# A factorization kernel on one core: bias loaded last, two load queues, P2 in its own bank, 12-bit parts by adding DMAs, unscaled banks

## The chip, the cores and the metric

The kernel runs on one core of a Trainium2 chip. The metric is the device time of one execution in microseconds (us). The core's engines are TensorE (PE, matmuls; PEld is its weight load), VectorE (DVE), ScalarE (ACT), GpSimd (POOL) and SyncE (SP, which here only issues transfers). Matmul results land in PSUM banks, everything else lies in SBUF or in device memory.

## The reference

```python
out_lin = x @ lin_w.T + lin_b                       # x 1024x512, lin_w 512x512
xv = jnp.einsum('bf,efm->bem', x, weight)           # weight 64x512x512
zp = jnp.einsum('bf,efm->bem', jnp.square(x), jnp.square(weight))
interaction = 0.5 * jnp.sum(jnp.square(xv) - zp, axis=1)
return out_lin + interaction
```

All is fp32. Nearly all of the work is xv, 64 products of 1024x512 by 512x512, squared and summed over the 64. zp needs only the sum of the squared weights over e, so it is one product at the end.

## The kernel before, in words

**Seven products in place of eight.** Every large product is done as a 2x2 block product in the Strassen-Winograd form: seven block products P1 to P7 of sums of the blocks. The left operands are quarters of x (A11, A12, A22, also X1, X2, X4) and four sums of them (R5, R6, R3, R7, also X5, X6, X3, X7). The right operands are the weight quarters w11, w21, w22, a running sum T (which takes quarter after quarter and serves P5, P6 and P4), and w12 after w22 was added to it (P7).

**Stages.** First the linear part x @ lin_w.T (`one_level` in lines 485 to 513: matmuls L494 where it goes by k, L507 elsewhere), which runs in plain fp32 and leaves its four quarters in device memory (`lin_copy`, `lin_add`, `lin_store`). Then 32 half groups (16 groups of columns times two halves of NCB), each with the seven products in the order P1, P6, P2, P3, P7, next half group's P5, P4 (`ORDER`); their matmuls are L678. Last the tail, which multiplies the squares of x by the sums of the squared weights (`one_level` again, L507), adds the accumulated interaction and the linear part to it (`into`), and stores.

**A product of a half group** (`product`, line 670). Fp32 operands are split into 12-bit parts so that PE can take them in its faster fp32r type: H (leading), L (rest) and K (a combination of both that makes up for the cross terms). A product is a front, H·H and L·L, and a back, K·K, which comes `LAG` = 4 slots later; between them the bank is scaled by 1 + 2^-12 and takes its addend (`stt`, L349; `dve`, L355; L712). In half group 0 the products P1, P2, P4 (`PLAIN`) are done in plain fp32. The 12-bit parts of x (`x_pieces`, line 471) are made once; those of the weights (`split`, line 612) for every product: pH and pL by ACT (L343), then pL by a POOL subtraction (L361) or by a DMA that adds (L380), and pK by POOL.

**Banks.** Four double banks go round in a ring. Each product has two halves (of 256 rows of x each), each half with a double bank. So P4's second half takes the double bank that P7's second half had.

**What reads a bank.** After the back, `finish` (line 663) has ACT square the bank (sq<-bank) and DVE reduce it into acc. P7's bank has a second reader: DVE's w<-bank−p5 (lines 727 and following), the addend of P4. Two instructions of different engines that read the same bank run one after the other, in the order in which they are emitted.

**Order of the work.** Nothing is emitted directly. Every operation is put on a `Plan` with its cost on its engine and what it reads and writes. `deadlines` gives each its latest start, counted back from the chain of matmuls, whose order is fixed by their keys. `forward` then simulates the engines: each takes, of what is ready, the operation with the earliest latest start. Loads on SP are not issued more than `AHEAD` = 50 us before that. `order` repeats this 60 times with shifted due times (`urge`) and keeps the one that ends first; instructions are emitted in that order. `both` marks DVE instructions that share a port with POOL. `landing` tells the plan when a load at the start is taken to arrive.

Of the kernel before, what the change touches and what calls it, by code (L numbers as in the profile page):

```python
# [19 lines left out]
U = 2.0 ** -12  # L20
S = 2.0 ** 12
TRIM = 1.0 - 2.0 ** -13

PLAIN = (1, 2, 4)
LAG = 4
ORDER = (1, 6, 2, 3, 7, 5, 4)
SPLIT = {**dict.fromkeys(range(1, 8), "POOL"), 5: "DMA", 3: "DMA"}
SCALE = {1: "DVE", 5: "ACT"}
# [5 lines left out]
PE, DVE, ACT, POOL, SP = "PE", "DVE", "ACT", "POOL", "SP"  # L34
NONE = ""


class Plan:
    HOP = 0.3
    OWN = 0.05  # L40
    AHEAD = 50.0
    ROUNDS = 60
    SEED = 0
    DEPTH = 8
    YIELD = 0.0

    def __init__(self):
        self.ops = []
# [91 lines left out]
    def forward(self, chain):  # L140
# [3 lines left out]
        free = dict.fromkeys(pending, 0.0)  # L144
        running = dict.fromkeys(pending)
        times = [self.HOP]
        done, late, nxt, wire, held = [], 0.0, 0, [9.0], None

        def release(o):
            for e in o.costs:  # L150
# [24 lines left out]
        def pick(e, now):  # L175
            if e == PE:
                if nxt < len(chain):
                    o = chain[nxt]
                    if not left[o.n] and ready(o, PE) <= now + 1e-6:
                        return o  # L180
                return None
            at = {n: ready(ops[n], e) for n in pending[e]}
            for n in sorted((n for n in at if at[n] <= now + 1e-6),
                            key=lambda n: (ops[n].latest, n)):
                o = ops[n]
                if e == SP and o.latest - self.AHEAD > now + 1e-6:
                    heapq.heappush(times, o.latest - self.AHEAD)
                    return None
                until = now + o.costs[e]
                if not any(  # L190
                    now + 1e-6 < at[u] < until - 0.2
                    and ops[u].latest < o.latest
                    and ops[u].latest + late < until + 0.1
                    for u in at
                ):
                    return o
            return None
# [43 lines left out]
def kernel(  # L241
# [5 lines left out]
    lin_b: bass.AP,  # L247
    out: bass.AP,
):

# [87 lines left out]
    def f32(n):  # L338
        return buf[n].bitcast(F32)
# [60 lines left out]
    def landing(name, at):  # L400
        plan.add({SP: 0.0}, None, (), (name,), land=at - 2 * plan.HOP)
# [16 lines left out]
        for z in ks:  # L418
            landing((n, z % KH, c), at)

    load_x("A11", 0, 0, 1, 3.5)
    load_lw(nc.scalar, [0], 0, 3.5)
    load_x("A11", 0, 1, 2, 3.9)
    load_lw(nc.scalar, [1], 0, 5.2)
    load_x("A11", 1, 0, 2, 5.0)
    load_lw(nc.scalar, [2, 3], 0, 7.2)
    load_x("A12", 0, 0, 2, 6.4)
    load_x("A12", 1, 0, 2, 7.4)
    load_lw(nc.sync, [0, 1], 1, 8.4)
    load_lw(nc.sync, [2, 3], 1, 9.2)  # L430
    for at, (n, k) in enumerate((("A22", 0), ("A22", 1), ("A21", 0), ("A21", 1))):
        load_x(n, k, 0, 2, 10.0 + 0.8 * at)
    nc.scalar.dma_start(bias[:], lin_b)
    landing("bias", 9.5)
    nc.scalar.preload_act_table(AF.Square)

    def a_parts(*names):
# [31 lines left out]
    x_sum("R7", "A11", "A21", "a - b", ("R7",))  # L469
    x_sum("R3", "R6", "A12", "-a - b", ("R3",))  # L470
    def x_pieces(i):
        n, (h, l, k) = OPERAND[i], (f"X{i}{z}" for z in "HLK")
        act(buf[h], buf[n], AF.Copy, a_parts(n), (h,), scale=S * TRIM)
        stt(buf[l], buf[n], S, f32(h), ALU.subtract, a_parts(n) + (h,), (l,), 1024, True)
        stt(buf[k], f32(h), -U, f32(l), ALU.add, (h, l), (k,), 1024, True)

    for i in (5, 6, 3, 7, 1, 2, 4):
        x_pieces(i)
# [3 lines left out]
    def four():  # L482
        return [both_of(banks()) for _ in range(4)]
# [33 lines left out]
        r.update({p: (t[k], t_names[k]) for p, k in ((5, 1), (6, 2), (7, 3), (4, 4))})  # L517
        return r

    f1, f4, f3, f2 = four()  # L520
    zero = nc.const_aps.tensor(0.0, [P, N])
    for u in range(2):
        nc.tensor.matmul(
# [16 lines left out]
        dma(lin_dram[:, ts(c, 2), ts(h, H)], buf[n], ((n, 0), (n, 1)), (("lind", h, c),))  # L540

    one_level(1, lin_rhs, lhs, f1, True, -1000, True)
    for u in range(2):
        act(buf[f2[u]], buf[f1[u]], AF.Copy, (f1[u],), (f2[u],), 512)
    one_level(2, lin_rhs, lhs, f1, False, -990, True)
    lin_copy("L11", f1, 0, 1.0)
    lin_store("L11", 0, 0)
    one_level(4, lin_rhs, lhs, f4, True, -980)
    one_level(5, lin_rhs, lhs, f3, True, -970)
    buf["L22"] = buf["A21"]  # L550
    used(("L22", 0), ("L22", 1), *a_parts("A21"))
    lin_copy("L22", f3, 1, -1.0)
    one_level(6, lin_rhs, lhs, f2, False, -960)
# [5 lines left out]
    lin_copy("L12", f2, 1, -1.0)  # L559
    one_level(3, lin_rhs, lhs, f3, False, -950)  # L560
    lin_add("L12", f3, True)
    lin_store("L12", 0, 1)
    one_level(7, lin_rhs, lhs, f2, False, -940)
    lin_add("L22", f2, True)
    lin_store("L22", 1, 1)
    lin_add("L21", f2, False)
    lin_store("L21", 1, 0)


# [26 lines left out]
    def load_more(h, n, q):  # L596

        o = now[h, n]
        if h:
            dma_add(buf[o], src(h, q), (), (o,))  # L600
        else:
            i = now[h, QUAD[q]]
            pool(buf[o], buf[o], buf[i], False, (o, i), (o,))
# [24 lines left out]
    def prepare(h, p):  # L628
        if p == 5:
            load(h, "T", 0)  # L630
            if h:
                load_more(h, "T", 1)
                load(h, "w11", 0)
            load(h, "w12", 1)
            if not h:
                load_more(h, "T", 1)
                load(h, "w11", 0)
                load(h, "w22", 3)
                load(h, "w21", 2)
# [17 lines left out]
        return n if not h and p in PLAIN else split(n, SPLIT[p] if h else POOL)  # L657

    acc_name = {}
    value = {}  # L660
# [191 lines left out]
    one_level(6, right, left, f2, False, key + 8)  # L852
    for u in range(2):
        into(z, f2, True, u)
        n = o_name[0, 1]
        dve(buf[n, u], buf[n, u], buf[z, u], True, ((n, u), (z, u)), ((n, u),), 512, True)
    one_level(7, right, left, f2, False, key + 11)
    for u in range(2):
        into(y, f2, True, u)
# [3 lines left out]
        into(o_name[1, 0], f2, True, u)  # L863
    one_level(3, right, left, f4, True, key + 14)
    for u in range(2):
        into(o_name[0, 1], f4, True, u)
# [52 lines left out]
```

## Time and profile before

| | us |
|---|---|
| median of 3 runs | 1298.06 |
| lowest and highest of them | 1298.05, 1299.3 |
| profiled execution, its own time | 1299.58 |
| profiled execution, its span | 1297.6 |

The mean granted TensorE clock of the profiled execution is 0.999. In the rows that follow, a line such as "L343 ACT ACTIVATE sq<-bank" is a group of instructions by source line, engine, operation and tiles (output on the left). In a timeline row the first number is the start in us from the start of the span, the second the time it took, and the bracket at the end says how long the engine had been idle and what released it. In a table of waits stand the total in us, the number of waits and the longest. In the table by stretches each engine has its busy time and number of instructions, and the granted clock, the share of the DMA engines and GB/s follow. In the chain of waits, each row is a start, a duration and what the end of the program went through. Line 343 is every ACT instruction, 349 every `stt`, 355 every `dve`, 361 every `pool`, 368 every `reduce`, 375 every `dma`, 380 every `dma_add`, so tiles tell them apart. Several tiles have two names there: w, p, sq and T are also the homes of x's quarters and of the lin weights at the start.

### The profile page before, as it was taken

How to read it: one execution, taken by the hardware profiler on the slowest of the kernel's cores; microseconds unless marked ns; L12 is line 12 of the kernel's file. 1: busy time of each engine (PE TensorE's matmuls, PEld its weight loads, DVE VectorE, ACT ScalarE, POOL GpSimd, SP SyncE). 2: the span in 40 equal slices, each digit the busy share in tenths (PEclk: the TensorE clock that was granted, in tenths of full speed). 3: DMA queues.
4: the chain of work that ended last, by engine and by line, in shares of the span. 5: the costliest groups of instructions: out<-in, count | busy, mean ns of one | idle time of the engine just before them, and what ended most of it. 6: DMA issues, size and time to landing. Idle time of an engine off the chain costs nothing.

```text
span 1297.6 us, 15705 instructions
## 1 busy us (share of the span) xinstructions
PE 1280.1 (99%) x5484; PEld 1026.0 (79%) x5484; DVE 1086.7 (84%) x954; ACT 1011.9 (78%) x1071; POOL 1095.3 (84%) x590
## 2 busy tenths in 40 slices
PE   8999999999999999999999999999999999999997
PEld 4668888888888888888888888888888888888873
DVE  4699888888888888888888888888888889888884
ACT  5568788788777888877888887788888788888872
POOL 3659898898888899889889888888988888998891
PEclk9999999999999999999999999999999999999999
DMA  6366676757667666677766666767667676766866
GB/s 226 97 164 160 155 170 150 158 129 154 163 155 167 142 152 145 149 163 164 162 147 143 153 151 161 167 145 161 133 148 168 147 162 152 169 131 144 184 130 150
DMA packets 75998, 200.25 MB, mean 154 GB/s; under 512 B 23824, under 2 KB 25104, under 8 KB 75920
## 3 DMA queue, kind: packets, MB, share of 16 engines
q0 software_dynamic: 28512, 101.72, 44.0%
q1 hardware_dynamic: 45552, 94.91, 22.6%
q10 hardware_dynamic: 1856, 2.62, 0.6%
q8 instruction: 43, 0.70, 0.2%
q14 instruction: 35, 0.29, 0.1%
HBM read 158.34 MB, written 6.29 MB: 127 GB/s over the span
## 4 chain that ended last, share of the span: by engine, by line
PE 92%; DMA 3%; DVE 2%; ACT 1%; issue 1%; POOL 1%; SPq 0%; DVEq 0%; ACTq 0%; POOLq 0%
PE bank L678 89%; PE bank L507 3%; DMA T<-weight 1%; DMA w<-weight 1%; DMA w<-xT 0%; PE bank L494 0%; DVE w L355 0%; POOL pL L361 0%; ACT sq L343 0%; ACT wsq L343 0%; POOL pK L361 0%; ACT pL L343 0%; DVE bank L355 0%; ACT bank L343 0%; DVE bank L349 0%
## 5 line engine op out<-in xcount | busy, mean ns | idle before, releaser
L361 POOL TENSOR_TENSOR pK<-pH,pL 128x1024 fp32r<-128x1024 f32 x221 | 560.1, 2554 | 19.8 <-PE bank L678 10.8
L343 ACT ACTIVATE sq<-bank 128x1024 f32<-128x1024 f32 x256 | 261.5, 1022 | 112.8 <-DVE w L355 52.2
L368 DVE TENSOR_REDUCE acc<-sq 128x16 f32<-128x1024 f32 x256 | 306.9, 1211 | 10.7 <-ACT sq L343 10.7
L361 POOL TENSOR_TENSOR pL<-w,pL 128x1024 fp32r<-128x1024 f32 x95 | 240.3, 2530 | 13.8 <-ACT pL L343 11.8
L361 POOL TENSOR_TENSOR pL<-T,pL 128x1024 fp32r<-128x1024 f32 x64 | 155.0, 2422 | 97.2 <-ACT pL L343 95.7
L349 DVE SCALAR_TENSOR_TENSOR bank<-bank,w 128x1024 f32<-128x1024 f32 x190 | 233.0, 1226 | 3.4 <-PE bank L678 3.4
L355 DVE TENSOR_TENSOR w<-bank,p 128x1024 f32<-128x1024 f32 x128 | 156.7, 1224 | 54.6 <-PE bank L678 52.4
L349 DVE SCALAR_TENSOR_TENSOR bank<-bank,p 128x1024 f32<-128x1024 f32 x126 | 154.4, 1226 | 44.9 <-ACT p L343 35.9
L343 ACT ACTIVATE pL<-T 128x1024 fp32r<-128x1024 f32 x95 | 100.9, 1062 | 83.5 <-issue 44.2
L343 ACT ACTIVATE pL<-w 128x1024 fp32r<-128x1024 f32 x126 | 133.8, 1063 | 36.0 <-issue 29.6
L368 DVE TENSOR_REDUCE w_sum<-wsq 128x16 f32<-128x1024 f32 x128 | 155.2, 1213 | 7.9 <-ACT wsq L343 7.2
L343 ACT ACTIVATE wsq<-w 128x1024 f32<-128x1024 f32 x128 | 134.7, 1052 | 2.7 <-DVE w_sum L368 2.6
L343 ACT ACTIVATE p<-bank 128x1024 f32<-128x1024 f32 x128 | 130.1, 1018 | 8.4 <-PE bank L678 6.9
L343 ACT ACTIVATE pH<-w 128x1024 fp32r<-128x1024 f32 x126 | 133.0, 1055 | 0.0
L712 DVE TENSOR_SCALAR bank<-bank 128x1024 f32<-128x1024 f32 x62 | 76.4, 1232 | 54.8 <-PE bank L678 54.7
L343 ACT ACTIVATE pH<-T 128x1024 fp32r<-128x1024 f32 x95 | 100.0, 1052 | 0.0
L380 POOL DMA_DIRECT2D T<-weight x93 | 99.4, 1069 | 0.0
L678 PE MATMUL bank<-pH,X3H 128*128 128x512 f32 x256 | 78.9, 389 | 1.0 <-DVE w L355 1.0
L678 PE MATMUL bank<-pH,X7H 128*128 128x512 f32 x256 | 79.2, 390 | 0.4 <-ACT sq L343 0.3
L678 PE MATMUL bank<-pH,X5H 128*128 128x512 f32 x256 | 79.4, 391 | 0.0
L678 PE MATMUL bank<-pH,X2H 128*128 128x512 f32 x248 | 76.5, 389 | 2.7 <-ACT pH L343 2.7
L678 PE MATMUL bank<-pL,X7L 128*128 128x512 f32 x256 | 78.9, 389 | 0.0
(116 smaller groups left out, 2550.1 us busy)
## 6 DMA issues: line engine op xcount, KB each, us to landing
w<-weight SPq DMA_DIRECT2D x128, 512.0 KB, 5.6
T<-weight POOLq DMA_DIRECT2D x93, 512.0 KB, 7.4
T<-weight SPq DMA_DIRECT2D x32, 512.0 KB, 3.6
pL<-T POOLq DMA_DIRECT2D x31, 512.0 KB, 6.1
pL<-w POOLq DMA_DIRECT2D x31, 512.0 KB, 5.2
w<-weight POOLq DMA_DIRECT2D x31, 512.0 KB, 5.3
accd<-turned SPq DMA_DIRECT2D x64, 32.0 KB, 5.0
p<-lind SPq DMA_DIRECT2D x4, 512.0 KB, 4.7
```

Of the source, the lines that this page charges most:

```text
L343: nc.scalar.activation(o, i, func, bias=bias, scale=scale)
L349: return nc.vector.scalar_tensor_tensor(o, i, scalar, j, ALU.mult, op)
L355: return (nc.vector.tensor_sub if sub else nc.vector.tensor_add)(o, a, b)
L361: return (nc.gpsimd.tensor_sub if sub else nc.gpsimd.tensor_add)(o, a, b)
L368: lambda _: nc.vector.tensor_reduce(o, i.rearrange("p a (m e) -> p a m e", e=E), axis=AX.X, op=ALU.add),
L380: {POOL: 0.95}, lambda _: nc.gpsimd.dma_start(o, i, accum_op=ALU.add),
L507: nc.tensor.matmul(buf[bank[u]], b[:, k, ts(u, P)], a[:, k, :], start=first and k == 0, stop=k == KH - 1, skip_group_check=True,)
L678: nc.tensor.matmul(buf[bank, j], buf[x][:, k, ts(2 * half + j, P)], buf[w][:, k, :], start=first and k == 0, stop=k == KH - 1, skip_group_ ...
L712: plan.add({DVE: 1.2}, lambda _, o=o: nc.vector.tensor_scalar(o, o, 1 + U, None, ALU.mult), names, names)
```

## The change

It has five parts.

1. The loads at the start. All lin weights are loaded on ACT's queue, x on SP's, and the bias last on SP's. The times given to `landing` are changed to match.
2. The linear part. Level 2 (P2) has a bank of its own, f2, instead of being added on top of level 1's bank; the two ACT copies of f1 to f2 go, levels 6 and 7 go on in f1, and L11 takes P2 by two DVE additions of 512 columns. The tail does the same: the two negating ACT copies go, level 1 is added to the output with `into`, and wt[2] is negated in place of wt[3].
3. The parts of X. H is scaled by 2^12 less. L and K of X1, X2, X4 are made by an ACT copy and a DMA that adds, in place of a DVE instruction each; L of X5, X6, X3, X7 is made by a plain subtraction. The banks then hold 2^-12 of the product, so the Square takes a scale of 2^12, and half group 0's plain products are scaled by 2^-12 where they meet an addend or are copied.
4. Half group 0. T's three sums and w12 + w22 are made by a DMA that adds from device memory, as in the other half groups, in place of a POOL addition.
5. The plan. `AHEAD` goes from 50 to 20, a new `SOON` = 25 holds POOL's transfers back in the same way, and the first free time of the simulated wire goes from 9 to 12.

```diff
+X_SPLIT = {5: DVE, 6: DVE, 3: DVE, 7: DVE, 1: "DMA", 2: "DMA", 4: "DMA"}
+FIRST = dict.fromkeys(range(1, 8), "POOL")
...
-    AHEAD = 50.0
+    AHEAD = 20.0
+    SOON = 25.0
...
+                if e == POOL and o.move and o.latest - self.SOON > now + 1e-6:
+                    heapq.heappush(times, o.latest - self.SOON)
+                    continue
...
-    load_lw(nc.sync, [0, 1], 1, 8.4)
-    load_lw(nc.sync, [2, 3], 1, 9.2)
-    for at, (n, k) in enumerate((("A22", 0), ("A22", 1), ("A21", 0), ("A21", 1))):
-        load_x(n, k, 0, 2, 10.0 + 0.8 * at)
-    nc.scalar.dma_start(bias[:], lin_b)
-    landing("bias", 9.5)
+    load_lw(nc.scalar, [0, 1], 1, 7.6)
+    load_lw(nc.scalar, [2, 3], 1, 8.8)
+    load_x("A22", 0, 0, 2, 9.6)
+    load_x("A22", 1, 0, 2, 10.4)
+    load_x("A21", 0, 0, 2, 11.2)
+    load_x("A21", 1, 0, 2, 12.0)
+    nc.sync.dma_start(bias[:], lin_b)
+    landing("bias", 13.5)
...
-        act(buf[h], buf[n], AF.Copy, a_parts(n), (h,), scale=S * TRIM)
-        stt(buf[l], buf[n], S, f32(h), ALU.subtract, a_parts(n) + (h,), (l,), 1024, True)
-        stt(buf[k], f32(h), -U, f32(l), ALU.add, (h, l), (k,), 1024, True)
+        parts = a_parts(n)
+        act(buf[h], buf[n], AF.Copy, parts, (h,), scale=TRIM)
+        if X_SPLIT[i] == "DMA":
+            act(buf[l], buf[n], AF.Copy, parts, (l,), scale=-TRIM)
+            dma_add(f32(l), buf[n], parts, (l,))
+            act(buf[k], buf[n], AF.Copy, parts, (k,), scale=-U * TRIM)
+            dma_add(f32(k), f32(l), (l,), (k,))
+        else:
+            dve(buf[l], buf[n], f32(h), True, parts + (h,), (l,), 1024, True)
+            stt(buf[k], f32(h), -U, f32(l), ALU.add, (h, l), (k,), 1024, True)
...
-    f1, f4, f3, f2 = four()
+    f2, f4, f3, f1 = four()
...
     one_level(1, lin_rhs, lhs, f1, True, -1000, True)
-    for u in range(2):
-        act(buf[f2[u]], buf[f1[u]], AF.Copy, (f1[u],), (f2[u],), 512)
-    one_level(2, lin_rhs, lhs, f1, False, -990, True)
     lin_copy("L11", f1, 0, 1.0)
+    one_level(2, lin_rhs, lhs, f2, True, -990, True)
+    lin_add("L11", f2, False)
...
-        if h:
+        if h or MORE:
             dma_add(buf[o], src(h, q), (), (o,))
...
-    act(buf[sq], buf[bank], AF.Square, both_of(bank), (sq,))
+    act(buf[sq], buf[bank], AF.Square, both_of(bank), (sq,), scale=S)
...
-                    dve(o, o, buf[addend], False, (addend, *names), names, 1024)
+                    stt(o, o, U, buf[addend], ALU.add, (addend, *names), names, 1024)
...
-                act(buf[n], o, AF.Copy, names, (n,))
+                act(buf[n], o, AF.Copy, names, (n,), scale=U if plain else 1.0)
...
-    act(wt[3], wt[3], AF.Copy, wt_names[3], wt_names[3], 512, -1.0)
+    act(wt[2], wt[2], AF.Copy, wt_names[2], wt_names[2], 512, -1.0)
...
     one_level(1, right, left, f1, True, key)
     for u in range(2):
-        act(buf[f2[u]], buf[f1[u]], AF.Copy, (f1[u],), (f2[u],), 512, -1.0)
+        into(o_name[0, 0], f1, False, u)
...
-    one_level(2, right, left, f1, False, key + 20)
+    one_level(2, right, left, f2, True, key + 20)
     for u in range(2):
-        into(o_name[0, 0], f1, False, u)
+        into(o_name[0, 0], f2, False, u)
         store(0, 0, u)
```

Where the second and later levels of the linear part and the tail named f2 (levels 6 and 7) they now name f1, and the sign with which `into` adds them is turned where the operand or the negated sum is. `FIRST` gives every product of half group 0 POOL, as before. Lines of the changed kernel stand 9 to 19 further down: L343 is L352 there, L355 L364, L494 L513, L507 L526, L678 L696.

More of the change, by code (lines that the diff above doesn't have):

```diff
@@ L22 @@
 TRIM = 1.0 - 2.0 ** -13
+PE, DVE, ACT, POOL, SP = "PE", "DVE", "ACT", "POOL", "SP"
 PLAIN = (1, 2, 4)
@@ L27 @@
 SPLIT = {**dict.fromkeys(range(1, 8), "POOL"), 5: "DMA", 3: "DMA"}
+MORE = True
+X_SPLIT = {5: DVE, 6: DVE, 3: DVE, 7: DVE, 1: "DMA", 2: "DMA", 4: "DMA"}
+FIRST = dict.fromkeys(range(1, 8), "POOL")
 SCALE = {1: "DVE", 5: "ACT"}
@@ L32 @@
 PAIRS = {"p1": 2, "w": 2, "p5": 3}
-PE, DVE, ACT, POOL, SP = "PE", "DVE", "ACT", "POOL", "SP"
 NONE = ""
@@ L146, in forward @@
         times = [self.HOP]
-        done, late, nxt, wire, held = [], 0.0, 0, [9.0], None
+        done, late, nxt, wire, held = [], 0.0, 0, [12.0], None
         def release(o):
@@ L419, in load_lw @@
             landing((n, z % KH, c), at)
[L421 to L428, printed above, removed]
-    load_lw(nc.sync, [0, 1], 1, 8.4)
-    load_lw(nc.sync, [2, 3], 1, 9.2)
-    for at, (n, k) in enumerate((("A22", 0), ("A22", 1), ("A21", 0), ("A21", 1))):
-        load_x(n, k, 0, 2, 10.0 + 0.8 * at)
-    nc.scalar.dma_start(bias[:], lin_b)
-    landing("bias", 9.5)
+    load_x("A11", 0, 0, 1, 3.7)
+    load_lw(nc.scalar, [0], 0, 3.6)
+    load_x("A11", 0, 1, 2, 4.4)
+    load_lw(nc.scalar, [1], 0, 4.4)
+    load_x("A11", 1, 0, 2, 5.8)
+    load_lw(nc.scalar, [2, 3], 0, 6.2)
+    load_x("A12", 0, 0, 2, 6.9)
+    load_x("A12", 1, 0, 2, 8.0)
+    load_lw(nc.scalar, [0, 1], 1, 7.6)
[6 more added lines that the diff above has]
+    landing("bias", 13.5)
     nc.scalar.preload_act_table(AF.Square)
@@ L552 @@
     lin_copy("L22", f3, 1, -1.0)
-    one_level(6, lin_rhs, lhs, f2, False, -960)
+    one_level(6, lin_rhs, lhs, f1, False, -960)
     buf["L21"] = buf["lt0"]
@@ L558 @@
     used(("L12", 0), ("L12", 1), *lw_names[0, 0], *lw_names[0, 1])
-    lin_copy("L12", f2, 1, -1.0)
+    lin_copy("L12", f1, 1, -1.0)
     one_level(3, lin_rhs, lhs, f3, False, -950)
@@ L562 @@
     lin_store("L12", 0, 1)
-    one_level(7, lin_rhs, lhs, f2, False, -940)
-    lin_add("L22", f2, True)
+    one_level(7, lin_rhs, lhs, f1, False, -940)
+    lin_add("L22", f1, True)
     lin_store("L22", 1, 1)
-    lin_add("L21", f2, False)
+    lin_add("L21", f1, False)
     lin_store("L21", 1, 0)
@@ L656, in prepare @@
         n = now[h, RHS[p]]
-        return n if not h and p in PLAIN else split(n, SPLIT[p] if h else POOL)
+        return n if not h and p in PLAIN else split(n, SPLIT[p] if h else FIRST[p])
     acc_name = {}
@@ L851 @@
             act(buf[n, u], buf[f3[u]], AF.Copy, (f3[u],), ((n, u),), 512)
-    one_level(6, right, left, f2, False, key + 8)
+    one_level(6, right, left, f1, False, key + 8)
     for u in range(2):
-        into(z, f2, True, u)
+        into(z, f1, False, u)
         n = o_name[0, 1]
         dve(buf[n, u], buf[n, u], buf[z, u], True, ((n, u), (z, u)), ((n, u),), 512, True)
-    one_level(7, right, left, f2, False, key + 11)
+    one_level(7, right, left, f1, False, key + 11)
     for u in range(2):
-        into(y, f2, True, u)
+        into(y, f1, False, u)
         n = o_name[1, 1]
@@ L862 @@
         store(1, 1, u)
-        into(o_name[1, 0], f2, True, u)
+        into(o_name[1, 0], f1, False, u)
     one_level(3, right, left, f4, True, key + 14)
```

## The prediction

> **What bounds the kernel now.** I read the page's busy shares first, then the table by stretches, then what TensorE (PE) waited for.
>
> ```profile
> span 1297.6 us, 15705 instructions
> PE 1280.1 (99%) x5484; PEld 1026.0 (79%) x5484; DVE 1086.7 (84%) x954; ACT 1011.9 (78%) x1071; POOL 1095.3 (84%) x590
> ...
> 200.00:400.00 200.00, 200.00 (x883) 164.95 (x882) 170.56 (x150) 163.40 (x173) 178.35 (x95) 1.00 0.68 152
> ...
> PE bank L678 <- ACT pH L343: 2.7, 1, 2.7
> PE bank L507 <- DVE w L355: 1.6, 2, 0.8
> PE bank L494 <- DMA w<-xT: 1.6, 1, 1.6
> PE bank L494 <- ACT bank L343: 1.3, 2, 0.7
> ...
> PE bank L678 <- DVE w L355: 1.0, 1, 1.0
> ...
> PE bank L494 <- ACT wsq L343: 0.8, 1, 0.8
> PE bank L678 <- ACT sq L343: 0.3, 1, 0.3
> ```
>
> PE is busy 99% of the span, and all of the stretch from 200 to 400 us: 883 matmuls in 200 us are 0.2265 us each, at full granted clock (1.00). DVE, ACT and POOL have 11 to 18% to spare there. So the change can only gain where PE waits, and the wait table lists how little that is: some 3.7 us at the start (L494), 4.0 us in the half groups (L678), 1.6 us behind DVE in the last stage (L507). The built programs have the same matmuls in the same order, so no matmul time goes away. It loses wherever a new wait enters the loop, times its repeats.
>
> **The change part by part.**
>
> *Start (own bank for P2, loads, bias last).* The chain of waits at the start:
>
> ```profile
> 8.18 1.55 PE bank L494 x6
> ...
> 9.75 0.59 ACT bank L343
> ...
> 10.38 0.71 PE bank L494 x2
> ...
> 11.12 0.59 ACT bank L343
> ...
> 11.75 3.30 PE bank L494 x14
> ...
> 15.08 0.70 ACT wsq L343
> ...
> 15.82 0.70 PE bank L494 x2
> ```
>
> Three times PE stops for ACT to read a bank before level 2 or 4 may write it. The gaps are 10.38 − 9.73, 11.75 − 11.09 and 15.82 − 15.05, so 0.65 + 0.66 + 0.77 = 2.1 us, and each restart costs about 0.12 more (shown below), so 2.4. With P2 in a bank of its own no copy stands ahead of a matmul, and all three gaps go. The two added DVE additions for L11 wait for nobody on PE's path. The first matmul still needs the x load that it waited 1.6 us for; x keeps its place on SP's queue. Bounds: −4.0 if that load also comes 1.6 earlier, −1.5 if the lin weights, now all behind one queue, give 0.9 back. I take **−2.5**.
>
> *T sums of half group 0 by DMA.*
>
> ```profile
> 18.27 2.92 POOL L361 TENSOR_TENSOR T<-T,w 128x1024 f32<-128x1024 f32 x1 [17.82 <-DMA w<-weight]
> ...
> 22.36 2.36 POOL L361 TENSOR_TENSOR pL<-T,pL 128x1024 fp32r<-128x1024 f32 x1 [1.17 <-ACT pL L343]
> ...
> 33.69 16.02 PE bank L678 x56
> ...
> T<-weight POOLq DMA_DIRECT2D x93, 512.0 KB, 7.4
> L380 POOL DMA_DIRECT2D T<-weight x93 | 99.4, 1069 | 0.0
> ```
>
> Before, T was ready at 18.27 + 2.92 = 21.2 and P5's first matmul came at 33.69. A DMA add issued no later than 18.3 lands 7.4 later, at 25.7; ACT's copy and POOL's subtraction (1.06 and 2.36) put pL at 29.2 or, with the second ACT copy ahead of it, 30.2. PE would now want it at 33.69 − 2.5 = 31.2. So it costs **0**, with 1 to 2 us of cover; what is behind it is the first rival at the start, below. POOL gains 4 × 2.6 and loses 10 issues of 1.07 (four sums, six X pieces), which is nothing where POOL is off the path.
>
> The Trainium skill, *DMA: Bandwidth & Descriptors*, section "Anatomy of one DMA — SWDGE (gpsimd) path", fits such a transfer as 2.0 us plus bytes over 436e3 per us, 3.2 us for 512 KB. By that the sum would be ready near 21.5 and the cover would be 5 us or more. The row says 7.4, more than twice that, and I go by the row.
>
> *X1, X2, X4 pieces by ACT and DMA; half group 0 and 1.*
>
> ```profile
> 59.97 1.21 DVE L355 TENSOR_TENSOR w<-bank,p 128x1024 f32<-128x1024 f32 x1
> 61.23 0.73 PE L678 MATMUL bank<-pH,X3H 128*128 128x512 f32 x2 [1.02 <-DVE w L355]
> ...
> 77.88 1.22 DVE X4L L349
> ...
> 82.48 1.14 DVE X2L L349
> ...
> 83.64 8.98 DMA w<-weight
> ...
> 94.77 0.73 PE L678 MATMUL bank<-pH,X2H 128*128 128x512 f32 x2 [2.72 <-ACT pH L343]
> ...
> 147.26 0.73 PE L678 MATMUL bank<-pH,X7H 128*128 128x512 f32 x2 [0.33 <-ACT sq L343]
> ...
> 948.44 0.74 PE L678 MATMUL bank<-pH,X7H 128*128 128x512 f32 x2
> ```
>
> Six DVE instructions of 1.2 us leave, two of them (X4L, X2L) directly ahead of the weight load of 83.64 whose landing holds pH and the matmul at 94.77. With them gone the DVE queue is 7 us shorter by then; both stalls go: 1.02 + 2.72, and 0.12 each for the restart, **−4.0** (at worst −2.5: in the built order the loads of half group 1 have only some 5 us between issue and need). The small stall at 147.26 is behind a late T sum; the built order now puts the sums further ahead: 0.33 + 0.12, and as much at 948.44, where the longer first row (0.74) shows a restart: **−0.85** (0 at the other end). The added ACT copies (six of 1.05) and DMA adds have tens of us. The changed scales alter no instruction's length.
>
> *What the new plan times reorder.* SP and POOL moves are held back to 20 and 25 us before their due time, and the scheduler then emits the other engines in another order. The weight loads keep 15 us or more of lead in the loop, above the 8.98 of the slowest row. One pair turns round. P7's second half leaves a bank that two engines read: ACT's Square (sq<-bank) and DVE's subtraction (w<-bank,p). The built program has the Square first in 30 of the half groups, before in two; whichever is emitted second waits for the first.
>
> ```profile
> 612.19 1.07 PE L678 MATMUL bank<-pK,X7K 128*128 128x512 f32 x4
> 612.82 1.05 ACT L343 ACTIVATE wsq<-w 128x1024 f32<-128x1024 f32 x1
> ...
> 613.30 1.22 DVE L355 TENSOR_TENSOR w<-bank,p 128x1024 f32<-128x1024 f32 x1 [0.37 <-PE bank L678]
> ...
> 614.61 1.03 ACT L343 ACTIVATE sq<-bank 128x1024 f32<-128x1024 f32 x1 [0.75 <-DVE w L355]
> ...
> 615.83 0.61 PE L678 MATMUL bank<-pH,X4H 128*128 128x512 f32 x2
> ...
> 1071.35 1.03 ACT L343 ACTIVATE sq<-bank 128x1024 f32<-128x1024 f32 x1 [0.56 <-PE bank L678]
> ...
> 1072.41 1.23 DVE L355 TENSOR_TENSOR w<-bank,p 128x1024 f32<-128x1024 f32 x1 [0.19 <-ACT sq L343]
> ...
> 1223.47 1.05 ACT L343 ACTIVATE pH<-w 128x1024 fp32r<-128x1024 f32 x1
> 1224.42 1.02 ACT L343 ACTIVATE bank<-bank 128x1024 f32<-128x1024 f32 x1
> ```
>
> At 612 the order is DVE (613.30 to 614.52), then ACT (614.61 to 615.64), and PE's P4, second half, which takes that same bank, starts at 615.83 unhindered: 0.19 us to spare. The period at 1071 has the other order, and the DVE row names the Square as what it waited for. In the changed program the Square stands behind wsq: wsq at 612.82, the next ACT instruction 0.95 later (1223.47 to 1224.42) at 613.77, DVE 1.06 behind that (1071.35 to 1072.41) at 614.83, done 1.22 later at 616.05, PE 0.05 after (59.97 + 1.21 to 61.23) at 616.10. That is 0.27 after 615.83. A restarted pair takes 0.73 instead of 0.61 (61.23, 94.77), so 0.39 in each of 30 half groups: **+11.7**. Bounds: 0, as the period at 1071 nearly shows, where no wsq stood between and PE lost no whole wait; 0.39 as worked out, and 0.5 if ACT has one more small delay. I take 0.39 since every instruction in it has its row and PE has no slack to win it back with. Behind the late DVE instruction stand the reduction of sq and P4's additions, which have the same 0.39 given to them by PE.
>
> The Trainium skill, *PSUM — Partial Sum Buffer*, section "Terms", says two engines on one bank and quadrant at once are a collision, reads against reads included. By it all 30 pairs must run one after the other, as the row at 1072.41 does; readers free to overlap would make this part 0.
>
> *Tail.*
>
> ```profile
> 1292.84 1.20 DVE p L355 x2
> ```
>
> By the built order five DVE additions instead of four follow the last matmul, at 0.60 each: **+0.6** (0 to +2, since the last transpose is now behind four more additions, 2.4 us, under some 12 us of cover). The stage's two waits on DVE stay.
>
> Sum: −2.5 − 4.0 − 0.85 + 0.6 + 11.7 = **+4.95**. The profiled execution took 1299.58 (span 1297.6 and 1.98 around it), 1.52 above the median 1298.06; on the median the forecast is **1303.0**.
>
> **The rivals.**
> (a) *The turned pair is free*, because DVE or ACT gets to it early enough, as at 1071. Then only the gains stay: 1298.06 − 2.5 − 4.0 − 0.85 + 0.6 = 1291.3, faster. For it: the two cases of before cost next to nothing. Against: wsq stands between in the new order, and 0.19 us of room does not hold 1.06. 16%.
> (b) *Half price*: the wait is there without the restart's 0.12, 0.27 × 30 = 8.1, so 1299.4; or ACT comes 0.1 earlier to both. Within the bound of no change. 21%.
> (c) *A late start*: T's DMA add takes 10 us rather than 7.4 because the start's other loads share the engines; pL is then past 31.2, PE waits 1 to 2 us, and ACT's copies behind pL<-T keep lin banks too: 1303 + 2 to 4, 1306. It decides from a landing later than 26.7. 10%.
> (d) *A second wait in the loop*: POOL moves are issued only 25 us ahead, and a pK that waits for a DMA add lands 0.1 late in each half group: +3, 1306. 8%.
> (e) *The forecast*, 1301 to 1305: 45%.
>
> **How the numbers follow.** A measurement of this kernel tells about 0.2%, 2.6 us, from no change: faster is under 1295.5, slower over 1300.7. Faster is (a), 0.16, and 0.01 from large start gains: 0.17. Same is (b), 0.21, less a little: 0.20. Slower is (c), (d), (e): 0.63. The range reaches from the lower part of (b) to (c): 1296.5 to 1306.5, leaving (a) out; the forecast's own is 1301 to 1305.
>
> **What would show it.** PE rows for bank<-pH,X4H waiting on DVE w L355, near 30 times, 0.2 to 0.4 each, make the main step right; none of them makes it wrong and (a) true. DVE w<-bank,p should name ACT sq as releaser about 30 times more than before. At the start, P1 to P4 of L494 without an ACT wait, and P5's first matmul near 31.2; the waits of 2.7 and 1.0 gone from the table. It is wrong as a whole if PE's wait table in the loop is still empty, or if a wait on POOL pK or a DMA leads it.

## The result and the profile after

The changed kernel takes **1307.25 us** (median of 6 runs, 1306.71 to 1307.42) beside 1298.24 us for the kernel before on the same chip: a ratio of **1.0067, 95% interval [1.0054, 1.0079]**, 9.0 us slower. It was forecast slower, at 1303.0 within 1296.5 to 1306.5: the direction came out, the size is past the range.

The page of the changed kernel, its table by stretches (PE, PEld, DVE, ACT, POOL with their busy us and instructions, then granted clock, DMA share, GB/s), and PE's table of waits:

```profile
span 1305.6 us, 15688 instructions
PE 1285.5 (98%) x5484; PEld 1025.1 (79%) x5484; DVE 1083.1 (83%) x952; ACT 1016.2 (78%) x1073; POOL 1094.8 (84%) x596
...
200.00:400.00 200.00, 199.43 (x876) 163.20 (x875) 170.38 (x148) 161.88 (x172) 175.72 (x95) 1.00 0.69 150
...
PE bank L513 <- DMA w<-xT: 1.9, 1, 1.9
PE bank L696 <- DMA pL<-T: 0.8, 1, 0.8
PE bank L526 <- ACT p L352: 0.8, 1, 0.8
```

PE did 876 matmuls in the stretch from 200 to 400 us where it had done 883. Seven matmuls of 0.2265 us are 1.6 us lost in about five half groups, yet PE's wait table has not one row for it: each wait is so short that the modelled end of the matmul ahead covers most of it, and PE still reads as 199.43 of 200 us busy. The loss is seen by counting matmuls, in DVE's waits, and in those of PE's weight loads. Three rows of before, then the same three of after (us in total, times, longest):

```profile
DVE acc L368 <- ACT sq L343: 10.7, 14, 1.6
...
PEld bank L678 <- DVE w L355: 1.7, 2, 1.4
...
DVE w L355 <- ACT sq L343: 1.4, 2, 1.2
```

```profile
DVE acc L377 <- ACT sq L352: 62.9, 80, 2.3
...
DVE w L364 <- ACT sq L352: 19.2, 30, 0.6
PEld bank L696 <- DVE w L364: 16.1, 30, 0.5
```

DVE's subtraction w<-bank,p waited for ACT's Square 30 times, against 2 before, and DVE's reductions of the Squares stood waiting for 62.9 us against 10.7: both are now earlier in DVE's queue than their data. The row of the weight loads (PEld) names the releaser, DVE's w, and the count, 30; its 16.1 us are waits of weight loads, not matmul time lost. To see where the time went, the same matmul is looked up in both timelines (before, then after):

```profile
33.12 1.02 PE L678 MATMUL bank<-pH,X5H 128*128 128x512 f32 x2
...
158.41 0.39 PE L678 MATMUL bank<-pH,X4H 128*128 128x512 f32 x1
...
1226.50 0.67 PE L678 MATMUL bank<-pH,X4H 128*128 128x512 f32 x2
```

```profile
30.90 1.03 PE L696 MATMUL bank<-pH,X5H 128*128 128x512 f32 x2
...
153.06 0.50 PE L696 MATMUL bank<-pH,X4H 128*128 128x512 f32 x1
...
1230.96 0.73 PE L696 MATMUL bank<-pH,X4H 128*128 128x512 f32 x2
```

| stage | after against before, us |
|---|---|
| first matmul of P5 | −2.2 |
| to 155 us | −5.4 |
| from there to 1230 us (28 half groups) | +9.8, now +4.5 behind |
| the rest, to the end of the span (1305.6 − 1297.6 = +8.0) | +3.5 |

The profiled execution of before (1299.58) was 1.3 above its median, that of after (1307.42) 0.2: that is the rest of the 9.0, about 1.

One half group of after, in the middle of the loop:

```profile
572.28 1.03 ACT L352 ACTIVATE sq<-bank 128x1024 f32<-128x1024 f32 x1 [1.06 <-DVE w L364]
572.58 1.07 PE L696 MATMUL bank<-pK,X7K 128*128 128x512 f32 x4
...
573.20 1.05 ACT L352 ACTIVATE wsq<-w 128x1024 f32<-128x1024 f32 x1
573.34 1.22 DVE L377 TENSOR_REDUCE acc<-sq 128x16 f32<-128x1024 f32 x1 [1.16 <-ACT sq L352]
...
574.15 1.02 ACT L352 ACTIVATE sq<-bank 128x1024 f32<-128x1024 f32 x1
...
575.20 1.23 DVE L364 TENSOR_TENSOR w<-bank,p 128x1024 f32<-128x1024 f32 x1 [0.64 <-ACT sq L352]
...
576.48 0.73 PE L696 MATMUL bank<-pH,X4H 128*128 128x512 f32 x2
```

From X7K (572.58) the Square comes at 1.57, the subtraction at 2.62, P4's second half at 3.90; the prediction had 1.58, 2.64 and 3.91. What it did not look at is the row at 573.34: DVE has the reduction of the *first* half's Square in its queue, idles 1.16 us for it, and is taken until 574.56. Before, the reduction at that place was of an older Square, done by 612.9, and the subtraction started as soon as the bank was full.

The tail of before, DVE's last transpose and what hangs on it:

```profile
1277.57 0.42 ACT L737 ACTIVATE acc<-acc 128x256 f32<-128x256 f32 x1 [3.30 <-DVE acc L368]
...
1279.09 0.44 DVE L740 STREAM_TRANSPOSE turned<-acc 128x256 f32<-128x256 f32 x1
...
1283.16 1.76 POOL L380 DMA_DIRECT2D p<-accd  x2 [11.82 <-DMA accd<-turned]
...
1293.35 0.69 DVE L355 TENSOR_TENSOR p<-p,w 128x512 f32<-128x512 f32 x1
```

The same in after, then the end of its chain of waits:

```profile
1282.12 0.42 ACT L755 ACTIVATE acc<-acc 128x256 f32<-128x256 f32 x1 [3.30 <-DVE acc L377]
1283.06 0.69 DVE L364 TENSOR_TENSOR w<-w,bank 128x512 f32<-128x512 f32 x1 [0.97 <-PE bank L526]
...
1288.22 0.44 DVE L758 STREAM_TRANSPOSE turned<-acc 128x256 f32<-128x256 f32 x1
...
1292.59 1.76 POOL L389 DMA_DIRECT2D p<-accd  x2 [19.38 <-DMA out<-p]
...
1300.60 0.69 DVE L364 TENSOR_TENSOR p<-p,w 128x512 f32<-128x512 f32 x1 [1.87 <-DMA p<-accd]
```

```profile
1290.46 2.05 DMA out<-p
1293.13 7.44 DMA p<-accd
```

acc is ready at 1282.54. The transpose waits until 1288.22 behind additions that wait for matmuls of the last stage; the store, POOL's add and its 7.44 us to land follow, and the last output is held until 1300.60, after DVE idled 1.87 us for it. PE had begun its last matmul at 1295.5. From the end of that matmul to the end of the span it took 6.1 us in before and 9.5 in after.

### The profile page after: what moved, and what is told of

Same layout as the page of the kernel before. It is cut to its first block, busy times and chain, and to the rows that moved or that the text cites. A ratio compares the mean times of both kernels' runs of the same rounds, so it can differ in the third digit from the quotient of the medians.

```text
span 1305.6 us, 15688 instructions
## 1 busy us (share of the span) xinstructions
PE 1285.5 (98%) x5484; PEld 1025.1 (79%) x5484; DVE 1083.1 (83%) x952; ACT 1016.2 (78%) x1073; POOL 1094.8 (84%) x596
## 4 chain that ended last, share of the span: by engine, by line
PE 66%; DMA 10%; POOL 7%; issue 6%; ACT 5%; DVE 5%; ACTq 0%; SPq 0%; POOLq 0%; DVEq 0%
PE bank L696 64%; DMA T<-weight 5%; POOL pK L370 5%; DVE w L364 4%; DMA pL<-T 4%; ACT sq L352 3%; PE bank L526 2%; POOL pL L370 2%; ACT pL L352 1%; DMA p<-accd 1%; ACT wsq L352 1%; POOL T L389 0%; DMA w<-xT 0%; PE bank L513 0%; POOL pL L389 0%
## 5 line engine op out<-in xcount | busy, mean ns | idle before, releaser
L370 POOL TENSOR_TENSOR pK<-pH,pL 128x1024 fp32r<-128x1024 f32 x221 | 575.9, 2624 | 24.7 <-DMA pL<-T 14.9
L377 DVE TENSOR_REDUCE acc<-sq 128x16 f32<-128x1024 f32 x256 | 310.5, 1213 | 65.3 <-ACT sq L352 62.9
L352 ACT ACTIVATE sq<-bank 128x1024 f32<-128x1024 f32 x256 | 261.1, 1020 | 124.1 <-PE bank L696 80.2
L370 POOL TENSOR_TENSOR pL<-w,pL 128x1024 fp32r<-128x1024 f32 x95 | 250.2, 2634 | 35.0 <-ACT pL L352 35.0
L370 POOL TENSOR_TENSOR pL<-T,pL 128x1024 fp32r<-128x1024 f32 x64 | 158.3, 2474 | 73.6 <-ACT pL L352 72.5
L364 DVE TENSOR_TENSOR w<-bank,p 128x1024 f32<-128x1024 f32 x128 | 156.7, 1224 | 54.1 <-PE bank L696 34.9
L358 DVE SCALAR_TENSOR_TENSOR bank<-bank,p 128x1024 f32<-128x1024 f32 x128 | 157.2, 1228 | 37.5 <-ACT p L352 29.8
L352 ACT ACTIVATE pL<-T 128x1024 fp32r<-128x1024 f32 x95 | 100.6, 1059 | 74.1 <-issue 41.4
L352 ACT ACTIVATE pL<-w 128x1024 fp32r<-128x1024 f32 x126 | 133.1, 1056 | 26.6 <-PE bank L696 24.2
L352 ACT ACTIVATE p<-bank 128x1024 f32<-128x1024 f32 x128 | 130.5, 1020 | 21.3 <-PE bank L696 21.2
L352 ACT ACTIVATE wsq<-w 128x1024 f32<-128x1024 f32 x128 | 134.6, 1052 | 0.2 <-DVE w_sum L377 0.2
L352 ACT ACTIVATE pH<-w 128x1024 fp32r<-128x1024 f32 x126 | 132.7, 1053 | 0.2 <-DMA w<-weight 0.2
L389 POOL DMA_DIRECT2D T<-weight x96 | 102.7, 1080 | 14.9 <-DMA T<-weight 14.6
L352 ACT ACTIVATE pH<-T 128x1024 fp32r<-128x1024 f32 x95 | 99.9, 1051 | 0.0
L696 PE MATMUL bank<-pH,X4H 128*128 128x512 f32 x248 | 80.1, 404 | 3.4
L696 PE MATMUL bank<-pL,X5L 128*128 128x512 f32 x256 | 78.9, 390 | 0.8 <-DMA pL<-T 0.8
L696 PE MATMUL bank<-pH,X5H 128*128 128x512 f32 x256 | 79.2, 391 | 0.0
L696 PE MATMUL bank<-pL,X7L 128*128 128x512 f32 x256 | 78.8, 389 | 0.0
L696 PE MATMUL bank<-pL,X6L 128*128 128x512 f32 x256 | 78.8, 389 | 0.0
```

The costliest lines, as they stand in the source:

```text
L352: nc.scalar.activation(o, i, func, bias=bias, scale=scale)
L358: return nc.vector.scalar_tensor_tensor(o, i, scalar, j, ALU.mult, op)
L364: return (nc.vector.tensor_sub if sub else nc.vector.tensor_add)(o, a, b)
L370: return (nc.gpsimd.tensor_sub if sub else nc.gpsimd.tensor_add)(o, a, b)
L377: lambda _: nc.vector.tensor_reduce(o, i.rearrange("p a (m e) -> p a m e", e=E), axis=AX.X, op=ALU.add),
L389: {POOL: 0.95}, lambda _: nc.gpsimd.dma_start(o, i, accum_op=ALU.add),
```

## The experiments

Medians of the kernel before ran from 1298.24 to 1300.78 from chip to chip, so each kernel is compared by its ratio to before on its own chip. Times in the third column are that ratio times 1298.24.

| run | ratio to before [95%] | on the scale of before = 1298.2 |
|---|---|---|
| the change | 1.0067 [1.0054, 1.0079] | 1306.9 |
| pair_back | 1.0187 [1.0173, 1.0201] | 1322.5 |
| reduce_back | 1.006 [1.0046, 1.0074] | 1306.0 |
| sub_front | 1.0 [0.9991, 1.0009] | 1298.2 |
| before_turned | 1.0107 [1.0093, 1.0121] | 1312.1 |
| tail_up | 1.0047 [1.0034, 1.006] | 1304.3 |
| pair_tail | 1.017 [1.0157, 1.0184] | 1320.3 |
| full | 0.9989 [0.998, 0.9997] | 1296.8 |
| ahead_50 | 1.0004 [0.9995, 1.0014] | 1298.8 |
| x_by_dve | 0.9982 [0.9973, 0.9991] | 1295.9 |
| late_tail | 0.9973 [0.9962, 0.9984] | 1294.7 |
| plan_alone | 1.0189 [1.0173, 1.0205] | 1322.8 |
| pair_in_plan | 1.0252 [1.0226, 1.0278] | 1331.0 |

The first theory was that of the prediction: the 30 turned pairs cost the loop, the late transpose the tail. To leave all else as it was, these edits take the finished plan of a kernel and move single operations in its emission order.

**The pair turned back (pair_back).**

```diff
+    made = plan.order()
+    for square_op, w_op in pairs_of_7:          # sq<-bank and w<-bank,p of one half of P7
+        at = {o.n: i for i, (o, _) in enumerate(made)}
+        if at[square_op.n] < at[w_op.n]:
+            made.insert(at[square_op.n], made.pop(at[w_op.n]))
```

> The changed kernel with its own plan; only the emission order of 30 pairs is turned back: in P7's second half DVE's w<-bank,p stands ahead of ACT's sq<-bank again. Theory A (the turned pair costs PE 0.28 + 0.11 us in each of 30 half groups): every wait of P4's second half goes, the loop gains 10 to 11.5, so 1296.5 (1295.5 to 1297.5) beside 1307.2. Theory B (the moves held back to 20 and 25 us and the added DMA adds load the loop, and the pair only shows the slack that is missing anyway): another wait takes its place, less than half comes back, 1302 or more.

Neither came: it is 16 us slower than the change. One half group of it:

```profile
579.47 1.22 DVE L377 TENSOR_REDUCE acc<-sq 128x16 f32<-128x1024 f32 x1 [1.16 <-ACT sq L352]
580.61 1.22 DVE L364 TENSOR_TENSOR w<-bank,p 128x1024 f32<-128x1024 f32 x1
581.91 1.03 ACT L352 ACTIVATE sq<-bank 128x1024 f32<-128x1024 f32 x1 [1.53 <-DVE w L364]
...
582.99 0.73 PE L696 MATMUL bank<-pH,X4H 128*128 128x512 f32 x2 [0.50 <-ACT sq L352]
```

The subtraction cannot start before 580.61, since the reduction of the first Square is ahead of it on DVE; the Square then waits for it until 581.91, and PE is held longer than with the Square first. So with that reduction where it is, the turned pair was the better order, and my theory of a single pair fell. The new one (A2) is two orders together: the reduction put DVE's subtraction late, and the Square went ahead because of it. That the planner chose the Square for this reason is a guess; no run looked into its choice.

**The other two corners (reduce_back, sub_front).** In reduce_back the reduction goes behind the subtraction and the Square stays first; in sub_front the subtraction goes ahead of both.

> The changed kernel with its own plan; only the reduction of the first half's Square is put behind w<-bank,p on DVE, the second Square stays ahead of it. Theory A2: the subtraction still waits for the second Square, which ends at the same time, so the wait of 0.39 per half group stays whole: 1307 (1306 to 1308), PE's rows bank<-pH,X4H with 0.28 and 0.11 as before. Were the reduction alone the cause, 1296.

> The changed kernel with its own plan; in P7's second half DVE's w<-bank,p goes ahead both of ACT's sq<-bank and of DVE's own reduction of the first half's Square. Theory A2 (two orders together: DVE's queue has the reduction of the first half's Square ahead of the subtraction, which waits for ACT, and the planner put the second Square first because DVE was taken; turned back alone the Square only waits longer): all 30 waits of P4's second half go, 11.4 less, 1296 (1295 to 1297.5) beside 1307.2. Theory B2 (the freed queue meets another wait, as it did when the pair alone was turned back): 1302 or more.

```diff
+    for z in range(1, len(pairs_of_7), 2):
+        square_op, w_op = pairs_of_7[z]
+        earlier = plan.ops[pairs_of_7[z - 1][0].n + 1]     # the reduction of the first half's Square
+        at = {o.n: i for i, (o, _) in enumerate(made)}
+        if at[square_op.n] < at[w_op.n] and at[earlier.n] < at[w_op.n]:
+            made.insert(at[w_op.n], made.pop(at[earlier.n]))
```

That is reduce_back; sub_front does the move of pair_back first and then this one.

reduce_back leaves all 30 waits, as A2 has it: the subtraction still starts right after the Square ended, and PE's matmul still takes 0.72.

```profile
613.54 1.02 ACT L352 ACTIVATE sq<-bank 128x1024 f32<-128x1024 f32 x1
...
614.59 1.23 DVE L364 TENSOR_TENSOR w<-bank,p 128x1024 f32<-128x1024 f32 x1 [3.01 <-ACT sq L352]
...
615.87 0.72 PE L696 MATMUL bank<-pH,X4H 128*128 128x512 f32 x2
```

sub_front takes all the waits of P4 away. Each order alone is worth nothing or less; both together are worth 8.7 us. But A2 had promised 11.4. What is left stands at P1:

```profile
577.98 1.02 ACT L352 ACTIVATE p<-bank 128x1024 f32<-128x1024 f32 x1
...
579.09 0.70 PE L696 MATMUL bank<-pH,X1H 128*128 128x512 f32 x2
```

P1's second half takes the bank that ACT empties into p until 579.00, and now waits for it a little in each half group. The queues behind the moved instructions were laid out for the other order, so B2 was right in part.

**Only the pair, in the kernel before (before_turned).** The inverse of pair_back, in the plan of before, for the second halves.

```diff
+    for square_op, w_op in pairs_of_7[1:-1:2]:
+        at = {o.n: i for i, (o, _) in enumerate(made)}
+        i, j = at[w_op.n], at[square_op.n]
+        if i < j:
+            made.insert(j, made.pop(i))
```

> The kernel before with its own plan; only the emission order of P7's second half is turned in the half groups: ACT's sq<-bank ahead of DVE's w<-bank,p. Nothing else of the change is in it. Theory A: PE waits for DVE at P4's second half in 30 half groups, 0.37 to 0.39 each, 1298.2 + 11.4 = 1309.6 (1308 to 1310.5). Theory B: the kernel before has the slack, 1299.5 or less.

```profile
620.78 1.02 ACT L343 ACTIVATE sq<-bank 128x1024 f32<-128x1024 f32 x1
...
621.83 1.22 DVE L355 TENSOR_TENSOR w<-bank,p 128x1024 f32<-128x1024 f32 x1 [1.89 <-ACT sq L343]
...
623.11 0.74 PE L678 MATMUL bank<-pH,X4H 128*128 128x512 f32 x2
```

DVE idles 1.89 us for the Square, and PE loses 0.37 to 0.40 us against before in each half group of the loop, the price of the prediction. The whole is some 2 us above what was expected: PE has two more waits of over 1 us, near 85 and 1240 us, and behind its wait of 2.58 us at 95 us the granted clock stood at 0.50 until 99.4. So the turned order by itself is enough to make a loss of this size, with no other part of the change present.

**The tail (tail_up, pair_tail).**

```diff
+    turn_15 = {o.n for o in last_turn}           # the last transpose and its four stores
+    moved = [x for x in made if x[0].n in turn_15]
+    made = [x for x in made if x[0].n not in turn_15]
+    at = next(i for i, (o, _) in enumerate(made) if o is last_mul) + 1
+    made[at:at] = moved
```

> The changed kernel with its own plan; only the last group's transpose and the four stores of accd behind it are emitted right after ACT's scaling of acc, ahead of DVE additions that wait for the last stage's matmuls. Theory A (the last transpose at 1288.22 sets when the adds from accd land, 1300.58, and these set the end): the end is again some 6 us after PE's last matmul instead of 9.5, 1304.0 (1303.3 to 1304.7). Theory B (the fifth DVE addition and the stores' queue set the end): no more than 0.6 less, 1306.6 or more.

2.6 us less by the ratio, but the two intervals overlap, so the trace is the better witness: the span ends 6.6 us behind the end of PE's last matmul, where the change took 9.5 and before 6.1. The end of its chain of waits is PE and then DVE again, with no transfer in it:

```profile
1283.12 12.30 PE bank L526 x28
1295.44 1.90 DVE p L364 x3
```

> Both of these edits together. Theory A: the two are apart in time and add up, 1307.2 - 10.7 - 3.2 = 1293.3 (1292 to 1294.5), which is under the kernel before. Theory B: 1299 or more, not under the kernel before by more than 0.2%.

pair_tail is 2.2 below pair_back, and its span ends 6.6 us behind PE's last matmul beside 8.8 there, so the tail's part adds to what the loop does; the sum was off because of the loop's.

**Everything moved by hand (full).** sub_front, tail_up, and at the start ACT's second copy of L12 directly behind level 6 (the edit of sub_front is called front in the text that follows).

```diff
     lin_copy("L12", f1, 1, -1.0)
+    l12_copy = plan.ops[-2:]
...
+    j = at[l12_copy[1].n]
+    i = max(at[n] for n in (l12_copy[0].n, *l12_copy[1].deps) if n in at) + 1
+    made.insert(i, made.pop(j))
```

> The edit of front, the earlier last transpose, and at the start ACT's second copy of L12 put right behind level 6, ahead of the copies of X3, X2 and T that stood before it. Theory A2: 1307.2 - 11.4 - 2.6 - 0.9 = 1292.3 (1291 to 1294), at the start PE's 0.76 us wait for ACT p before level 7 gone. Theory B2: 1299 or more.

It reaches 1296.8, under the kernel before, but not 1292.3: the loop keeps the small wait of sub_front. At the start the 0.76 us before level 7 are gone, and a wait of 1.3 for ACT pH came before X6H instead.

**Other plans for the same work.** Five kernels let the planner order again. Theory A3 in their texts is A2 carried over to them: the loop's loss is the order of the three instructions, the tail's the late transpose, and both go when the planner itself orders them well. The first three are the changed kernel with one thing told otherwise:

```diff
-    AHEAD = 20.0
+    AHEAD = 50.0
```

> The changed kernel as it is with one constant put back, AHEAD = 50. In the built program 127 of 128 subtractions stand ahead of the Square, the reduction stands behind, and the last transpose has 15 DVE instructions behind it instead of 11. Theory A2 (the order that the plan happens to come out with decides, not a part's work): 1293.5 (1292 to 1296). Theory B2 (late loads themselves or the added DMA adds cost): over 1299.

```diff
-    def dma_add(o, i, reads, writes, move=2.75):
+    def dma_add(o, i, reads, writes, move=2.75, land=2.5):
...
-                          if g * MG // P == ch), ((n, u),), 1.4)
+                          if g * MG // P == ch), ((n, u),), 1.4, 7.5)
```

> The changed kernel with only the landing of the adds from accd put right in the plan (7.5 us), nothing said of the pair. The built order has the Square first in 1 of 128 cases, as it comes out of this draw. Theory A3: as pair_in_plan in loop and tail, 1293.5 (1292 to 1296), since it is the order that counts and not how it came about.

```diff
-X_SPLIT = {5: DVE, 6: DVE, 3: DVE, 7: DVE, 1: "DMA", 2: "DMA", 4: "DMA"}
+X_SPLIT = dict.fromkeys(range(1, 8), DVE)
```

> The changed kernel with X1, X2, X4 split on DVE again (the first half of part 3 undone). The built order has the Square first in 4 of 128 cases and 15 instructions behind the last transpose. If the step of the prediction holds that X2L and X4L on DVE kept the load ahead of X2's first matmul late, PE waits again some 2.7 us before bank<-pH,X2H near 90 us, and the kernel is at 1296; if the loads are placed by the plan anyway, that wait is under 0.5 and the kernel is at 1293.5.

ahead_50 has next to no wait in the loop (it wins back 9.3 us there) and loses some 6 at the start, where ACT pH and POOL pL come late. late_tail, which tells the planner only that the adds from accd land later, has loop, tail and most of the start right, and is **0.27% faster than the kernel before**, the best of all; it still has a wait of 2.9 us near 94 us. x_by_dve is also faster than before, and the wait of 2.7 us at X2H, which the prediction had put on X2L and X4L, does not come back with them on DVE. Three unrelated edits thus each undid the turned order, so no single part of the change is shown to cause it.

plan_alone is the kernel before with the plan constants of part 5; pair_in_plan is late_tail with the subtraction put on the plan ahead of the Square, and one read more:

```diff
-        act(buf[sq], buf[bank], AF.Square, both_of(bank), (sq,), scale=S)
+        act(buf[sq], buf[bank], AF.Square, (*both_of(bank), *behind), (sq,), scale=S)
```

where `behind` is w for P7, so that the Square has to follow the subtraction.

> The kernel before with part 5 of the change alone (AHEAD 20, SOON 25, wire 12). The built order has the Square first in 2 of 128 cases, as before. Theory A3: the later moves themselves cost nothing in the loop, within 2 us of before, no wait of PE in the loop. Were the held-back moves the cause of the loop's loss, 5 us or more slower.

> The changed kernel with two edits to what the planner is told: the Square of P7's banks reads w as well, so that it must follow the subtraction, and the adds from accd are taken to land after 7.5 us instead of 2.5. In the built order the subtraction is ahead in all 128 cases, no reduction of the same half group's first Square stands ahead of it, the last transpose has 16 DVE instructions behind it, and ACT's order at the start is that of the changed kernel. Theory A3 (the loop's loss is the order of three instructions, the tail's the late transpose, and both go if the planner itself orders them, since all that depends on them is then ordered with them): no wait of PE between 110 and 1260 us, the start as in the changed kernel, 1307.2 - 11.4 - 2.6 = 1293.2 (1292 to 1295), or 0.4% under the kernel before on the same chip. Theory B3 (the changed loads and DMA adds leave so little room that a small wait of 0.1 to 0.15 per half group stays whatever the order, as in sub_front): 1297 or more, within 0.2% of before.

Both came out far from what was expected: 25 and 33 us slower than before. PE's table and one half group of plan_alone:

```profile
PE bank L682 <- ACT p L347: 14.3, 18, 3.3
```

```profile
671.53 1.50 POOL L384 DMA_DIRECT2D T<-weight  x1
671.67 1.04 ACT L347 ACTIVATE p<-bank 128x1024 f32<-128x1024 f32 x1
...
674.92 1.06 ACT L347 ACTIVATE pL<-T 128x1024 fp32r<-128x1024 f32 x1 [2.21 <-DMA T<-weight]
...
676.84 1.00 ACT L347 ACTIVATE p<-bank 128x1024 f32<-128x1024 f32 x1
...
677.89 0.74 PE L682 MATMUL bank<-pH,X1H 128*128 128x512 f32 x2 [1.25 <-ACT p L347]
```

The T sum was issued so late that ACT stood 2.21 us before pL<-T; the copy p<-bank, which P1's second half needs, is behind that in ACT's queue, and PE waits for it, up to 3.3 us. ACT stood 34.4 us in all for such sums, against 17.6 in before. pair_in_plan has the same picture (14 waits for ACT p, 15.3 us; ACT stood 40.6 us for T sums), and 7 waits of PE for the DMA add pL<-w, 6.5 us, besides. So part 5 alone is dear in the kernel before, by a wait that the changed kernel does not have: theory A3 fell there. That the hold of 25 us on POOL's transfers is what makes the T sum late is argued, not shown: no run changed the hold alone, and late_tail has the same hold without that wait. What is shown is that what a part costs in the loop depends on the order that comes out with it, and small edits to what the planner is told moved the kernel from 1294.7 to 1331.0 with the same matmuls.

## Why the prediction was right or wrong

- **What bounds the kernel; a new wait in the loop costs its repeats.** Right, it is the largest term, and not by luck: the Square, the subtraction and the matmul came within 0.02 us of where the prediction put them, counted from X7K. Stalls in P4's second half in the trace of after: 30 times, 8.27 us before the first matmul of the half and 3.30 at the second, 11.57 in all; the forecast had +11.7. The 0.85 of old stalls went as forecast.
- **Why it arises.** Incomplete. "Whichever is emitted second waits for the first" is right: in after the Square ends at 575.17 and the subtraction starts at 575.20, in pair_back the subtraction ends at 581.83 and the Square starts at 581.91. The Trainium skill's *PSUM — Partial Sum Buffer*, section "Terms", counts two engines at one bank and quadrant at once as a collision, reads included, and these rows, one after the other, agree. But the prediction took the pair for a free choice. The Square first is by itself enough for the loss (before_turned, reduce_back); the reduction ahead of the subtraction is enough for a larger one (pair_back); only with both put back does it go (sub_front).
- **Tail, +0.6, "under some 12 us of cover".** This is the step that failed. It measured +3.5; tail_up gives 2.6 of it back by the ratio, 2.9 by the way from PE's last matmul to the end of the span. The 12 us were counted from the transpose to the last additions, without what lies between: a store, POOL's issue, a transfer. In before, that way took from 1279.09 to a landing at 1289.32, and the last addition that needs it ran at 1293.35: 4.0 us of cover, not 12. And four additions that wait for matmuls put the transpose 5.7 us behind acc, where before had 1.1, so it moved by 4.6 us, not by 2.4.
- **Start, −2.5.** The three gaps went as forecast (level 4 starts at 13.11 against 16.36, −3.25). But 0.9 came back before level 7, so the term came out at −2.2: ACT's second copy of L12 stood behind copies for X3, X2 and T. "The added ACT copies have tens of us" was wrong for what queues behind them. The 0.3 by which the term missed says little: with the same order at the start, P5's first matmul came at 29.65 in tail_up and at 31.07 in reduce_back, as PE's wait for the first x load went from 0.3 to 1.6 us.
- **T's sums, 0.** Right: the add landed 7.3 us after its issue (22.36 − 15.02), as the row of before had it and not the 3.2 that the prediction estimated from the fit in the Trainium skill's *DMA: Bandwidth & Descriptors*, section "Anatomy of one DMA — SWDGE (gpsimd) path".
- **Half groups 0 and 1, −4.0.** Both stalls went, −4.0 with their restarts; new ones of 0.8 (DMA pL<-T at 106 us) and 0.2 (ACT p at 81 us), with theirs, took about 1.2 back. The cause given for the second stall, DVE's queue, is not borne out (x_by_dve).
- **From the profiled execution to the median.** The sum was applied to 1298.06 although the stalls were read from an execution 1.5 us longer. That is about 1 us of the miss. What made that execution longer was not looked into; one thing that varies is the wait for the first x load, 1.6 us in it and 0.7 in before_turned, which has the same start.
- **What would show it.** PE's wait table was the wrong place: it stayed empty in the loop with the step true, although the prediction had named that as the sign that it is wrong as a whole. DVE's waits (30, forecast about 30) were the right one, and the waits of PE's weight loads (PEld, 30).

In sum: forecast +4.95, measured +9.0; the tail is 2.9 of the difference, the start 0.3, the step from the profiled execution to the median about 1. What lies between start and tail came out 0.2 lower than forecast (−3.1 and +9.8 against −4.0, −0.85 and +11.7).

## What to carry to other kernels

Where a planner emits the instructions, read the built order before and after on every engine, and ask of each instruction that moved what stands ahead of it in its own queue: the pair had visibly turned round, but turning only it back made things worse, because another instruction had moved ahead of it. Count cover to the end of the chain (issue, landing, next engine), not to the end of the covered interval. And before a change is judged, let the planner draw a few orders: here the same matmuls span 36 us from the best order to the worst, more than any part of it was meant to bring.

## What the runs showed of the hardware

After some long waits PE came back at half its clock. In late_tail, PE waited 2.90 us until 97.1 us; the table by stretches shows the granted clock (third from the right) at 0.50 from 97 to 103 us, and at 1.00 later:

```profile
97.13 1.22 PE L696 MATMUL bank<-pL,X3L 128*128 128x512 f32 x2 [2.90 <-DMA pL<-w]
```

```profile
97.00:103.00 6.00, 5.87 (x14) 4.61 (x15) 2.89 (x4) 2.08 (x2) 6.00 (x3) 0.50 1.06 215
104.00:112.00 8.00, 8.00 (x37) 6.63 (x36) 6.14 (x7) 6.07 (x7) 6.42 (x4) 1.00 0.54 165
```

14 matmuls in 6 us instead of 26: some 15 matmuls each took 0.20 us more, so the wait of 2.9 cost 3 us again. The length of the wait does not decide it alone. The clock also stood at 0.50, for some 3.4 us, after waits of 1.85 us (plan_alone, at 101 us), 2.30 (pair_in_plan, at 666), 2.58 (before_turned, at 95), 3.04 (ahead_50, at 49) and 3.26 (plan_alone, at 207). It stayed at 1.00 after 2.72 in before (at 95) and after 2.93 in pair_in_plan (at 585). What decides it, no run here shows. The Trainium skill, *TensorE: Matmul & The Clock Gate*, section "Why this matters for your kernels", warns of idle gaps over some 3 us; here four shorter waits were enough, and two of nearly that length were not.
